# A two-cell recurrence on one core: normalization written in two halves, the cells' states summed ahead of the output product, and another order of a step

## The chip, the core and the metric

The program runs on one core of a Trainium2 chip. The metric is the device time of one execution in microseconds (us). The kernel before takes 3012.37 us, the median of three runs (3011.68 to 3013.71). The profiled execution spans 3003.6 us.

## What is computed

An image of 256 x 256 positions with 32 channels goes through four layers: a gated attention layer over an axis of length one (so that its softmax falls away), two Sobel layers, and a recurrence. The change touches the recurrence alone. It runs along the width: 256 steps t, over 256 sequences (one per row of the image), with two cells stacked (l = 0 and 1) of 128 hidden units:

```
z = x_t @ W_lat + b_lat
for j in range(2):
    zz = concatenate([z, h_all[j]]) @ W_cell[j] + b_cell[j]
    zz = group_norm(zz)            # 4 groups of 128: i, f, o, g
    i, f, o, g = split(zz, 4)
    c = sigmoid(f) * c_all[j] + sigmoid(i) * tanh(g)
    h = sigmoid(o) * tanh(c)
    z = z + h
x_hat = x_t + z @ W_out + b_out
```

Since z is the projected input plus h of both cells, x_hat needs (h0 + h1) @ W_out, and the rest is a product of x_t alone.

## The kernel before

The 256 sequences are held in two halves of 128 (h = 0 and 1), since a tile has 128 partitions. A **unit** is one cell on one half, written (l,h); a step has four units: (0,0), (0,1), (1,0), (1,1). A mean that group normalization would subtract is taken out of the weights beforehand, so what is left per unit is a mean square of each of the four groups and a division. The operations of a unit, by the names that the plan gives them and their lines in the profile:

- x (L702, TensorE, two products): the input's share of zz, for this unit of cell 1 and for a unit of cell 0 one or two steps on. i (L713): for cell 1, h of cell 0 in the same step times weights. m (L718): the unit's own h of the step before times weights. Each of i and m is 128x128 by 128x512 in float32, recorded as two matmul instructions.
- sq (L726, ScalarE): squares of zz, 512 columns. rd (L731, VectorE): their sums by group. pw (L734, GpSimd): the power -1/2 of 4 numbers per partition.
- nz (L738, VectorE): zn = zz times the four factors, 512 columns, out of the accumulator memory (PSUM).
- sg (L754, ScalarE): the sigmoid of i, f and o, 384 columns. tg (L756, ScalarE): the tanh of g.
- ig (L759, VectorE): c = i times g. fc (L763, GpSimd): f times the old c. c (L767, VectorE): c = c + fc, in place.
- th (L771, ScalarE): tanh of c. h (L774, VectorE): o times that. T (L777, TensorE): h transposed. e (L782): the copy out of PSUM into hT, on VectorE for cell 0 and on ScalarE for cell 1.

So every unit goes through TensorE, ScalarE, VectorE, GpSimd, VectorE, ScalarE, VectorE (with GpSimd beside it), ScalarE, VectorE and TensorE once per step, and the four units are staggered, so that each engine works on one unit while the others wait for another engine. The order in which the instructions stand in each engine's queue is written out by hand: PLAN gives each operation a time within the step, PERIOD is the distance of two steps, all operations of all 256 steps are sorted by time and emitted in that order. These times are not enforced on the chip. An engine takes its instructions strictly in the order of its queue, each as soon as what it waits for is there. In a planned time above PERIOD, the operation belongs to an earlier step than the one that runs at the same moment.

The output is written for blocks of four steps (emit, four parts, one per step): part 0 multiplies x_t of the block into px (L788); part 1 adds the four products of hT of cell 0 with W_out (L792); part 2 the four of cell 1, and then fin, ScalarE's copy of px with a bias (L801); part 3 transposes fin (pf, L808), VectorE copies that (st, L809), and every fourth block is stored. The emission stands at 0.90 of the step in the plan: after m(0,0) on TensorE, between sg(0,1) and tg(0,1) on ScalarE, and between c(1,0) and rd(1,1) on VectorE.

There is a second arm of the program for scales and shifts of the normalization that are not 1 and 0; with these inputs the first one (`plain`) runs.

Of the kernel before, what the change touches and what calls it, by code (L numbers as in the profile page):

```python
# [10 lines left out]
F32 = mybir.dt.float32  # L11
AF = mybir.ActivationFunctionType
# [4 lines left out]
S = 256  # L17
T = 256
C = 32
J = 4  # L20
NB = T // J
P = 128
H = 128
L = 2
# [490 lines left out]
def recurrent_weights(  # L515
# [114 lines left out]

PERIOD = 8.82
PLAN = {
    (0, 0): dict(m=0.0, sq=1.64, rd=2.4, pw=3.16, nz=4.25, sg=5.29, tg=5.72, fc=5.89, ig=6.1, c=6.55),
    (0, 1): dict(m=4.5, sq=6.14, rd=6.81, pw=7.57, nz=8.66, sg=9.61, tg=10.04, fc=10.21, ig=10.51),
    (1, 0): dict(x=10.17, i=11.42, m=12.42, sq=13.58, rd=14.3, pw=15.16, nz=16.47, sg=17.22, tg=17.65),
    (1, 1): dict(x=14.22, i=15.64, m=16.74, sq=17.9, rd=18.71, pw=19.48, nz=20.88, sg=21.63, tg=22.06),
}
PLAN[0, 0].update(th=6.9, h=7.43, T=7.8, e=8.27)  # L640
PLAN[0, 1].update(c=10.96, th=11.31, h=11.84, T=12.3, e=12.68)
PLAN[1, 0].update(fc=17.82, ig=18.1, c=18.45, th=19.07, h=19.56, T=20.12, e=20.48)
PLAN[1, 1].update(fc=22.23, ig=22.51, c=22.86, th=23.57, h=23.97, T=24.34, e=24.75)
EMIT = 27.36


def recurrence(tc, xa, out_nat, ident, weights, plain):

    nc = tc.nc
    wc, fx, gam, bet, e4, cst4, wout = weights  # L650
    XT = 2
    NX = 3
    ctx = ExitStack()
# [16 lines left out]

    up = ctx.enter_context(tc.tile_pool(name="unit", bufs=5))
    sp = ctx.enter_context(tc.tile_pool(name="state", bufs=2))
    hp = ctx.enter_context(tc.tile_pool(name="hid", bufs=10))
    op = ctx.enter_context(tc.tile_pool(name="outp", bufs=2))
    ps_zz = ctx.enter_context(tc.tile_pool(name="ps_zz", bufs=1, space=PSUM))
    ps_h = ctx.enter_context(tc.tile_pool(name="ps_h", bufs=2, space=PSUM))
# [2 lines left out]
    v = {}  # L679
    todo = []  # L680

    def at(when, what, *args):
        todo.append((when, len(todo), what, args))
# [10 lines left out]
    def project(l, h, t):  # L694

        if t >= T:
            return
        zz = v["zz", l, h] = ps_zz.tile([P, 4 * H], F32, name=f"zz{l}{h}")
        blk, j = divmod(t, J)
        rows = slice(l * X1, l * X1 + KX)  # L700
        x = xts[blk // XT % NX][rows, blk % XT, j, h * P : (h + 1) * P]
        nc.tensor.matmul(zz, lhsT=x, rhs=fx[rows, l, :], start=True, stop=l == 0 and t == 0)  # L702

    def one(name, l, h, t):
        seqs = slice(h * P, (h + 1) * P)
        get = lambda k: v[k, l, h]
        gates = lambda x, g: x[:, g * H : (g + 1) * H]
        four = lambda x: x.rearrange("p (g m) -> p g m", g=4)
        if name == "x":
            project(0, 1 - h, t + 1 + h)  # L710
            project(1, h, t)
        elif name == "i":
            nc.tensor.matmul(  # L713
                get("zz"), lhsT=v["hT", 0, t][:, seqs], rhs=wc[:, l, 0, :], start=False, stop=t == 0
            )
        elif name == "m":
            if t:
                nc.tensor.matmul(  # L718
                    get("zz"),
                    lhsT=v["hT", l, t - 1][:, seqs],  # L720
                    rhs=wc[:, l, 1, :],
                    start=False,
                    stop=True,
                )
        elif name == "sq":
            nc.scalar.activation(  # L726
                sqs[l, h][:, :, 0:H], four(get("zz")), AF.Square, scale=float(H**-0.5)
            )
        elif name == "rd":
            ve = v["ve", l, h] = up.tile([P, 4], F32, name="ve")  # L730
            nc.vector.tensor_reduce(ve, sqs[l, h], AX.X, ALU.add)  # L731
        elif name == "pw":
            rs = v["rs", l, h] = up.tile([P, 4], F32, name="rs")
            nc.gpsimd.tensor_tensor(rs, get("ve"), mhalf, ALU.pow)  # L734
        elif name == "nz":
            zn = v["zn", l, h] = up.tile([P, 4 * H], F32, name="zn")
            if plain:
                nc.vector.tensor_mul(  # L738
                    four(zn), four(get("zz")), get("rs").unsqueeze(2).to_broadcast([P, 4, H])
                )  # L740
                return
            for g in range(4):
                nc.vector.scalar_tensor_tensor(
                    gates(zn, g),
                    gates(get("zz"), g),
                    get("rs")[:, g : g + 1],
                    gates(gam[:, l, :], g),
                    ALU.mult,
                    ALU.mult,
                )  # L750
            nc.vector.tensor_add(zn, zn, bet[:, l, :])
        elif name == "sg":
            ga = v["ga", l, h] = up.tile([P, 4 * H], F32, name="ga")
            nc.scalar.activation(ga[:, 0 : 3 * H], get("zn")[:, 0 : 3 * H], AF.Sigmoid)  # L754
        elif name == "tg":
            nc.scalar.activation(gates(get("ga"), 3), gates(get("zn"), 3), AF.Tanh)  # L756
        elif name == "ig":
            c = v["cn", l, h] = sp.tile([P, H], F32, name=f"c{l}{h}")
            nc.vector.tensor_mul(c, gates(get("ga"), 0), gates(get("ga"), 3))  # L759
        elif name == "fc":  # L760
            if t:
                fc = v["fc", l, h] = up.tile([P, H], F32, name="fc")
                nc.gpsimd.tensor_mul(fc, gates(get("ga"), 1), get("c"))  # L763
        elif name == "c":
            c = get("cn")
            if t:
                nc.vector.tensor_add(c, c, get("fc"))  # L767
            v["c", l, h] = c
        elif name == "th":
            th = v["th", l, h] = up.tile([P, H], F32, name="th")  # L770
            nc.scalar.activation(th, get("c"), AF.Tanh)  # L771
        elif name == "h":
            hh = v["h", l, h] = up.tile([P, H], F32, name="h")
            nc.vector.tensor_mul(hh, gates(get("ga"), 2), get("th"))  # L774
        elif name == "T":
            pt = v["pt", l, h] = ps_h.tile([P, 4 * H], F32, name="pt")
            nc.tensor.transpose(pt[:, 0:P], get("h"), ident)  # L777
        elif name == "e":
            if h == 0:
                v["hT", l, t] = hp.tile([P, S], F32, name=f"hT{l}")  # L780
            copy = nc.scalar.copy if l else nc.vector.tensor_copy
            copy(v["hT", l, t][:, seqs], get("pt")[:, 0:P])  # L782

    def emit(blk, part):

        if part == 0:
            px = v["px"] = ps_x.tile([P, S], F32, name="px")
            nc.tensor.matmul(px, lhsT=e4, rhs=xa[:, blk, :], start=True, stop=False)  # L788
        elif part < 1 + L:
            l = part - 1  # L790
            for j in range(J):
                nc.tensor.matmul(  # L792
                    v["px"][j * C : (j + 1) * C, :],
                    lhsT=wout,
                    rhs=v.pop(("hT", l, blk * J + j)),
                    start=False,
                    stop=l == L - 1,
                )
            if l == L - 1:
                fin = v["fin"] = op.tile([P, S], F32, name="fin")  # L800
                nc.scalar.activation(fin, v["px"], AF.Identity, bias=cst4)  # L801
        else:
            if blk % 4 == 0:
                v["st"] = op.tile([P, 2, 4, P], F32, name="st")
            st = v["st"]
            pf = ps_x.tile([P, 2, P], F32, name="pf")
            for half in range(2):
                nc.tensor.transpose(pf[:, half, :], v["fin"][:, half * P : (half + 1) * P], ident)  # L808
            nc.vector.tensor_copy(st[:, :, blk % 4, :], pf)  # L809
            if blk % 4 == 3:  # L810
                w0 = (blk - 3) * J
                for half in range(2):
                    nc.sync.dma_start(
                        out=out_nat[:, half, w0 : w0 + 4 * J, :].rearrange("p w c -> p (w c)"),
                        in_=st[:, half].rearrange("p b m -> p (b m)"),
                    )

    for k in range(NB // XT):
        at(((k - NX + 1) * XT * J + 2.0) * PERIOD if k >= NX else -1e6, load, k)
    for h in range(2):  # L820
        at(-1e5, project, 0, h, 0)
    at(PLAN[1, 1]["x"] - PERIOD, project, 0, 0, 1)
    for t in range(T):
        for (l, h), ops in PLAN.items():
            for name, when in ops.items():
                at(t * PERIOD + when, one, name, l, h, t)
    for blk in range(NB):
        for part in range(L + 2):
            at((blk * J + J - 1 + part) * PERIOD + EMIT, emit, blk, part)
    todo.sort(key=lambda e: e[:2])  # L830
    with tc.manual_schedule():
# [44 lines left out]
```

## Time and profile before

| what | us |
|---|---|
| span of the profiled execution | 3003.6 |
| first normalization of the recurrence starts | 689.93 |
| last h of the recurrence | 2992.48 |
| one step on average: nz(0,0) of step 0 to step 255, 689.93 to 2973.61, by 255 | 8.956 |
| in 740 to 1500 us: TensorE busy | 733.26 of 760 |
| VectorE busy | 698.68 |
| ScalarE busy | 528.11 |
| GpSimd busy | 498.03 |

Steps are not equally long. From the starts of nz(0,0), steps 40 to 239, by the place of the step in its block of four (t mod 4), medians:

| from step t to t + 1, t mod 4 = | us | what of the emission falls in it |
|---|---|---|
| 1 | 8.59 | part 0 |
| 2 | 8.61 | part 1 |
| 3 | 9.48 | part 2 |
| 0 | 9.09 | part 3 |

The sum, 35.77 us a block, is what the recurrence is made of 64 times. In the profile "idle before" an instruction is the time that its engine stood still ahead of it, and behind the arrow stands what it waited for. The duration of an instruction on VectorE or ScalarE is longer than the distance to the next start: instructions that need not wait for each other overlap.

### The profile page before, as it was taken

Reading aid. Unit: us, or ns where it says so; the run is one execution under the profiler, and the core shown is the slowest. Engines: PE = TensorE matmul, PEld = TensorE weight load, DVE = VectorE, ACT = ScalarE, POOL = GpSimd, SP = SyncE. Lnnn points to the kernel's source line nnn. Section 1 sums busy time; section 2 is a strip of 40 time slices with the busy share of each in tenths; the row PEclk is TensorE's granted clock in tenths of the full one; section 3 lists DMA queues with packets and bytes.
Section 4 is the critical chain, followed back from the end, with each engine's and each line's share of the span. In section 5 each row is a group of like instructions: output and inputs, shape, how many; then the busy total and the mean of one; then the engine's idle time right before and its main releaser. Section 6 shows DMA issues by size and latency. Waiting matters only on the chain.

```text
span 3003.6 us, 39237 instructions
## 1 busy us (share of the span) xinstructions
PE 2830.3 (94%) x10209; PEld 1042.6 (35%) x10209; DVE 2646.4 (88%) x6572; ACT 1986.9 (66%) x5393; POOL 1718.6 (57%) x2272
## 2 busy tenths in 40 slices
PE   7899898988999999999999999999999999999997
PEld 4433333332333333333333333333333333333332
DVE  5778798986999999999999999999999999999997
ACT  5355486755666666676666766676666666666665
POOL 2300055636666666666666666666666666666665
PEclk9899999988999999999999999999999999999999
DMA  3000000001000000000000000000000000000000
GB/s 128 1 1 1 1 1 1 1 15 24 11 16 8 15 9 15 8 15 8 15 8 15 8 16 7 17 15 8 16 8 15 10 16 8 16 8 15 1 8 9
DMA packets 29314, 38.42 MB, mean 13 GB/s; under 512 B 5732, under 2 KB 22149, under 8 KB 29080
## 3 DMA queue, kind: packets, MB, share of 16 engines
q1 hardware_dynamic: 27392, 33.57, 3.9%
q8 instruction: 84, 1.38, 0.2%
q10 hardware_dynamic: 888, 1.95, 0.2%
q14 instruction: 150, 1.23, 0.1%
q0 software_dynamic: 800, 0.30, 0.0%
HBM read 10.63 MB, written 8.39 MB: 6 GB/s over the span
## 4 chain that ended last, share of the span: by engine, by line
PE 42%; DVE 39%; POOL 10%; issue 4%; ACT 2%; DVEq 0%; POOLq 0%; ACTq 0%
DVE ve L731 13%; PE zz L718 11%; POOL rs L734 9%; DVE zn L738 8%; PE zz L713 7%; DVE c L759 6%; DVE c L767 6%; PE pv L277 4%; PE pt L777 4%; PE pg L440 4%; PE pg L400 3%; PE px L792 2%; PE zz L702 2%; PE pg L302 2%; DVE h L774 2%
## 5 line engine op out<-in xcount | busy, mean ns | idle before, releaser
L734 POOL TENSOR_TENSOR rs<-ve,mhalf 128x4 f32<-128x4 f32 x1024 | 1036.6, 1012 | 281.5 <-DVE ve L731 237.1
L718 PE MATMUL zz<-wc,hT 128*128 128x512 f32 x2040 | 962.6, 594 | 1.2 <-DVE hT L782 1.2
L754 ACT ACTIVATE ga<-zn 128x384 f32<-128x384 f32 x1024 | 531.3, 519 | 468.0 <-DVE zn L738 467.5
L738 DVE TENSOR_TENSOR zn<-zz,rs 128x512 f32<-128x512 f32 x1024 | 701.1, 685 | 84.7 <-POOL rs L734 76.6
L763 POOL TENSOR_TENSOR fc<-ga,c 128x128 f32<-128x128 f32 x1020 | 466.8, 458 | 522.4 <-ACT ga L754 522.4
L731 DVE TENSOR_REDUCE ve<-sq 128x4 f32<-128x516 f32 x1024 | 697.2, 681 | 16.6 <-POOL sq L669 14.1
L726 ACT ACTIVATE sq<-zz 128x512 f32<-128x512 f32 x1024 | 606.3, 592 | 26.6 <-PE zz L718 14.3
L702 PE MATMUL zz<-fx,xt 33*128 33x512 f32 x2048 | 584.8, 643 | 11.5 <-DVE zn L738 8.2
L713 PE MATMUL zz<-wc,hT 128*128 128x512 f32 x1024 | 525.3, 595 | 0.0
L718 PEld LDWEIGHTS zz<-wc,hT 128*128 128x128 f32 x2040 | 359.6, 196 | 264.6 <-DVE hT L782 213.7
L771 ACT ACTIVATE th<-c 128x128 f32<-128x128 f32 x1024 | 311.4, 304 | 182.6 <-DVE c L767 177.9
L777 PEld LDWEIGHTS pt<-ident,h 128*128 128x128 f32 x1024 | 141.9, 139 | 804.8 <-DVE h L774 710.2
L777 PE MATMUL pt<-ident,h 128*128 128x128 f32 x1024 | 321.7, 314 | 87.6 <-DVE h L774 79.2
L767 DVE TENSOR_TENSOR c<-c,fc 128x128 f32<-128x128 f32 x1020 | 291.2, 286 | 55.9 <-DVE c L759 2.3
L759 DVE TENSOR_TENSOR c<-ga 128x128 f32<-128x128 f32 x1024 | 302.9, 296 | 38.7 <-ACT ga L756 38.6
L756 ACT ACTIVATE ga<-zn 128x128 f32<-128x128 f32 x1024 | 303.2, 296 | 0.0
L774 DVE TENSOR_TENSOR h<-ga,th 128x128 f32<-128x128 f32 x1024 | 292.0, 285 | 0.8 <-ACT th L771 0.8
L702 PEld LDWEIGHTS zz<-fx,xt 33*128 33x128 f32 x2048 | 156.1, 185 | 298.4 <-PE zz L718 226.3
L288 ACT ACTIVATE sg<-pg 128x512 f32<-128x512 f32 x256 | 132.1, 602 | 110.8 <-PE pg L277 110.8
L713 PEld LDWEIGHTS zz<-wc,hT 128*128 128x128 f32 x1024 | 183.3, 219 | 2.3 <-issue 2.3
L393 POOL TENSOR_TENSOR dh<-pp 128x512 f32<-128x512 f32 x64 | 99.4, 1553 | 115.6 <-DVE pp L380 98.9
L296 DVE TENSOR_TENSOR o<-pv,sg 128x512 f32<-128x512 f32 x256 | 155.4, 678 | 4.4 <-ACT sg L288 4.1
(147 smaller groups left out, 2306.8 us busy)
## 6 DMA issues: line engine op xcount, KB each, us to landing
xt<-xa SPq DMA_DIRECT2D x256, 64.0 KB, 2.0
nat<-in_x_dram SPq DMA_DIRECT2D x16, 512.0 KB, 8.3
out_dram<-st SPq DMA_DIRECT2D x32, 256.0 KB, 2.3
wc<-in_L_conv_W_cell_dram ACTq DMA_DIRECT2D x2, 512.0 KB, 4.1
kt<-in_consts_dram ACTq DMA_DIRECT2D x1, 832.0 KB
wv<-in_L_conv_Wv_dram POOLq DMA_DIRECT2D x4, 32.0 KB, 4.8
wg<-in_L_conv_Wg_dram POOLq DMA_DIRECT2D x4, 32.0 KB, 6.6
gamma<-in_L_conv_ln_gamma_dram POOLq DMA_DIRECT2D x4, 0.1 KB, 6.1
```

Of the source, the lines that this page charges most:

```text
L702: nc.tensor.matmul(zz, lhsT=x, rhs=fx[rows, l, :], start=True, stop=l == 0 and t == 0)
L713: nc.tensor.matmul(get("zz"), lhsT=v["hT", 0, t][:, seqs], rhs=wc[:, l, 0, :], start=False, stop=t == 0)
L718: nc.tensor.matmul(get("zz"), lhsT=v["hT", l, t - 1][:, seqs], rhs=wc[:, l, 1, :], start=False, stop=True,)
L726: nc.scalar.activation(sqs[l, h][:, :, 0:H], four(get("zz")), AF.Square, scale=float(H**-0.5))
L731: nc.vector.tensor_reduce(ve, sqs[l, h], AX.X, ALU.add)
L734: nc.gpsimd.tensor_tensor(rs, get("ve"), mhalf, ALU.pow)
L738: nc.vector.tensor_mul(four(zn), four(get("zz")), get("rs").unsqueeze(2).to_broadcast([P, 4, H]))
L754: nc.scalar.activation(ga[:, 0 : 3 * H], get("zn")[:, 0 : 3 * H], AF.Sigmoid)
L759: nc.vector.tensor_mul(c, gates(get("ga"), 0), gates(get("ga"), 3))
L763: nc.gpsimd.tensor_mul(fc, gates(get("ga"), 1), get("c"))
L767: nc.vector.tensor_add(c, c, get("fc"))
L777: nc.tensor.transpose(pt[:, 0:P], get("h"), ident)
```

## The change

Three things are changed, and the plan's numbers with them. The split is to let the gates begin on the first half of a unit's normalization, and to give the planner smaller pieces to place; the sum is to take products off TensorE and put an addition on GpSimd, which has more idle time.

- The normalization nz is written as two instructions of 256 columns: nz for the gates i and f, and n2 for o and g. The sigmoid is split in the same way: sg now takes i and f (256 columns), and a new so takes o (128 columns).
- A new hs on GpSimd adds hT of both cells (128x256), once per step. The output product then takes the sum: four products a block in place of eight, and the emission has three parts: x_t's product; the four products with fin behind them; the transposition with st.
- The plan has been made anew: PERIOD 8.74 for 8.82, and another order. On VectorE, ig of another unit stands between nz and n2 at two of the four places, and hT of cell 0 needs fewer buffers (6 for 10).

```
-PERIOD = 8.82
+PERIOD = 8.74
...
+        def half(i):
+            g = slice(2 * i, 2 * i + 2)
+            nc.vector.tensor_mul(
+                four(get("zn"))[:, g, :],
+                four(get("zz"))[:, g, :],
+                get("rs")[:, g].unsqueeze(2).to_broadcast([P, 2, H]),
+            )
...
+        elif name == "n2":
+            if plain:
+                half(1)
         elif name == "nz":
             zn = v["zn", l, h] = up.tile([P, 4 * H], F32, name="zn")
             if plain:
-                nc.vector.tensor_mul(
-                    four(zn), four(get("zz")), get("rs").unsqueeze(2).to_broadcast([P, 4, H])
-                )
+                half(0)
                 return
...
-            nc.scalar.activation(ga[:, 0 : 3 * H], get("zn")[:, 0 : 3 * H], AF.Sigmoid)
+            nc.scalar.activation(ga[:, 0 : 2 * H], get("zn")[:, 0 : 2 * H], AF.Sigmoid)
+        elif name == "so":
+            nc.scalar.activation(gates(get("ga"), 2), gates(get("zn"), 2), AF.Sigmoid)
...
+    def both(t):
+        hs = v["hs", t] = hp.tile([P, S], F32, name="hs")
+        nc.gpsimd.tensor_add(hs, *[v.pop(("hT", l, t)) if l else v["hT", l, t] for l in range(L)])
...
-                    rhs=v.pop(("hT", l, blk * J + j)),
+                    rhs=v.pop(("hs", blk * J + j)),
```

One half of a step in VectorE's queue, by the plans (a digit pair is the unit):

```
before: rd00 h01 nz11         e01 nz00 ig11      c11 rd10 ig00 h11 c00 | rd01
after:  rd00 h01 nz11 n2(11)  e01 nz00 ig11 n2(00) c11 rd10 ig00 h11 c00 | rd01
```

The other half is the same with the units rd01, h00, nz10, n2(10), e00, nz01, ig10, n2(01), c10, rd11, ig01, h10, c01. GpSimd's queue for one step is after the change: hs, fc01, pw11, pw00, fc11, fc00, pw10, pw01, fc10.

More of the change, by code (lines that the diff above doesn't have):

```diff
@@ L627, in recurrent_weights @@
     return (wc, fx, gam, bet, e4, cst4, wout), plain
-PERIOD = 8.82
+PERIOD = 8.74
 PLAN = {
[L635 to L638, printed above, removed]
-}
[L640 to L644, printed above, removed]
+    (0, 0): dict(m=0.0, sq=1.54, rd=2.37, pw=3.12, nz=4.21, n2=4.79, sg=5.28, tg=5.6, fc=5.76),
+    (0, 1): dict(m=4.47, sq=6.02, rd=6.74, pw=7.5, nz=8.59, n2=9.16, sg=9.54, tg=9.87, fc=10.03),
+    (1, 0): dict(x=9.98, i=11.34, m=12.35, sq=13.48, rd=14.14, pw=14.95, nz=16.32, n2=16.66),
+    (1, 1): dict(x=14.08, i=15.52, m=16.61, sq=17.75, rd=18.52, pw=19.27, nz=20.68, n2=21.04),
+}
+PLAN[0, 0].update(ig=6.03, c=6.47, so=6.56, th=6.83, h=7.36, T=7.72, e=8.28)
+PLAN[0, 1].update(ig=10.39, so=10.82, c=10.85, th=11.2, h=11.72, T=12.2, e=12.64)
+PLAN[1, 0].update(sg=16.8, tg=17.16, fc=17.29, so=17.36, ig=17.68, c=18.25, th=18.82, h=19.36)
+PLAN[1, 1].update(sg=21.18, tg=21.52, fc=21.66, so=21.73, ig=22.05, c=22.62, th=23.29, h=23.73)
+PLAN[1, 0].update(T=19.93, e=20.29)
+PLAN[1, 1].update(T=24.11, e=24.52, hs=26.48)
+EMIT = 27.09
 def recurrence(tc, xa, out_nat, ident, weights, plain):
@@ L672, in recurrence @@
     sp = ctx.enter_context(tc.tile_pool(name="state", bufs=2))
-    hp = ctx.enter_context(tc.tile_pool(name="hid", bufs=10))
+    hp = ctx.enter_context(tc.tile_pool(name="hid", bufs=6))
     op = ctx.enter_context(tc.tile_pool(name="outp", bufs=2))
@@ L774, in one @@
             nc.vector.tensor_mul(hh, gates(get("ga"), 2), get("th"))
+        elif name == "hs":
+            both(t)
         elif name == "T":
@@ L788, in emit @@
             nc.tensor.matmul(px, lhsT=e4, rhs=xa[:, blk, :], start=True, stop=False)
-        elif part < 1 + L:
-            l = part - 1
+        elif part == 1:
             for j in range(J):
@@ L794, in emit @@
                     lhsT=wout,
-                    rhs=v.pop(("hT", l, blk * J + j)),
+                    rhs=v.pop(("hs", blk * J + j)),
                     start=False,
-                    stop=l == L - 1,
+                    stop=True,
                 )
-            if l == L - 1:
-                fin = v["fin"] = op.tile([P, S], F32, name="fin")
-                nc.scalar.activation(fin, v["px"], AF.Identity, bias=cst4)
+            fin = v["fin"] = op.tile([P, S], F32, name="fin")
+            nc.scalar.activation(fin, v["px"], AF.Identity, bias=cst4)
         else:
@@ L827, in recurrence @@
     for blk in range(NB):
-        for part in range(L + 2):
+        for part in range(3):
             at((blk * J + J - 1 + part) * PERIOD + EMIT, emit, blk, part)
```

## The prediction

> **What bounds the kernel now.** I read the busy shares first, then the costliest groups, then the recurrence in order of time, and last the length of each step by its place in the block.
>
> ```profile
> PE 2830.3 (94%) x10209; PEld 1042.6 (35%) x10209; DVE 2646.4 (88%) x6572; ACT 1986.9 (66%) x5393; POOL 1718.6 (57%) x2272
> ...
> L734 POOL TENSOR_TENSOR rs<-ve,mhalf 128x4 f32<-128x4 f32 x1024 | 1036.6, 1012 | 281.5 <-DVE ve L731 237.1
> ...
> L738 DVE TENSOR_TENSOR zn<-zz,rs 128x512 f32<-128x512 f32 x1024 | 701.1, 685 | 84.7 <-POOL rs L734 76.6
> ```
>
> No engine is idle for long, but nz waits for the power, and the power for rd. The timeline of VectorE and GpSimd over one undisturbed half step shows how these interlock:
>
> ```profile
> 2158.46 0.69 DVE L738 TENSOR_TENSOR zn<-zz,rs 128x512 f32<-128x512 f32 x1 [0.19 <-POOL rs L734]
> ...
> 2159.07 0.28 DVE L759 TENSOR_TENSOR c<-ga 128x128 f32<-128x128 f32 x1
> ...
> 2159.45 0.29 DVE L767 TENSOR_TENSOR c<-c,fc 128x128 f32<-128x128 f32 x1
> ...
> 2159.66 0.68 DVE L731 TENSOR_REDUCE ve<-sq 128x4 f32<-128x516 f32 x1
> ...
> 2160.26 0.28 DVE L759 TENSOR_TENSOR c<-ga 128x128 f32<-128x128 f32 x1
> ...
> 2160.46 0.30 DVE L774 TENSOR_TENSOR h<-ga,th 128x128 f32<-128x128 f32 x1
> 2160.69 0.28 DVE L767 TENSOR_TENSOR c<-c,fc 128x128 f32<-128x128 f32 x1
> ...
> 2160.82 0.33 PE L777 MATMUL pt<-ident,h 128*128 128x128 f32 x1 [0.19 <-DVE h L774]
> ...
> 2160.89 0.68 DVE L731 TENSOR_REDUCE ve<-sq 128x4 f32<-128x516 f32 x1
> ...
> 2161.71 1.01 POOL L734 TENSOR_TENSOR rs<-ve,mhalf 128x4 f32<-128x4 f32 x1 [0.28 <-DVE ve L731]
> ...
> 2162.75 0.69 DVE L738 TENSOR_TENSOR zn<-zz,rs 128x512 f32<-128x512 f32 x1 [0.19 <-POOL rs L734]
> ```
>
> This is a closed loop of 4.29 us: nz to ig 0.61, ig to its c 0.38 (c waits for ig's result; unrelated small instructions start 0.20 apart), c to rd 0.21, rd to ig 0.60, ig to h 0.20, h to c 0.23, c to rd 0.20, then rd to nz by way of GpSimd 1.86. Twice that is 8.58; the undisturbed step has 8.59. So VectorE's queue with one power in it bounds a quiet step. TensorE is close behind: it stands still ahead of the transposition (0.19 here), and adding the starts (i 0.86, T about 0.15, m 0.86 twice, the two x products 1.06 and 0.09 ahead of them) gives some 4.05 a half, 8.1 a step.
>
> A block lasts 35.77 us, 4 x 8.59 is 34.36: emission costs 1.41 a block. Where it falls:
>
> ```profile
> 2155.20 0.47 ACT L801 ACTIVATE fin<-px,cst 128x256 f32<-128x256 f32 x1 [0.45 <-PE px L792]
> ...
> 2155.90 0.29 DVE L759 TENSOR_TENSOR c<-ga 128x128 f32<-128x128 f32 x1 [0.57 <-ACT ga L756]
> ```
>
> ```profile
> 2163.71 0.38 PE L808 MATMUL pf<-ident,fin 128*128 128x128 f32 x2
> ...
> 2163.75 0.29 DVE L767 TENSOR_TENSOR c<-c,fc 128x128 f32<-128x128 f32 x1
> ...
> 2164.12 0.43 DVE L809 COPY st<-pf 128x256 f32<-128x256 f32 x1
> ...
> 2164.47 0.68 DVE L731 TENSOR_REDUCE ve<-sq 128x4 f32<-128x516 f32 x1
> ```
>
> fin waits in ScalarE's queue for the output products with tg(0,1) behind it, and ig(0,1) waits for tg: pw(0,0) comes 2.01 us after pw(1,1) there (2155.41, 2157.42) in place of 1.29, so 0.72. Then st: c to rd takes 0.72 in place of 0.21, so 0.5: 0.35 its own slot, the rest the wait for pf. The remaining 0.19 is the first set of products (0.57 to 0.61 on TensorE, mostly inside its slack).
>
> [...] this trace has 1036 ns for an add of 512 columns (L389) and 458 for a product of 128 (L763).
>
> **The change, part by part.**
>
> Two halves of nz: [...] st, also 256 columns out of PSUM, has 425 in the trace, and 0.35 to the next start. So I take 0.34 a half: 0.68 in place of 0.61, 0.07 more, 0.28 a step of VectorE. It is on VectorE's queue, but only nz(0,0) and nz(0,1) lie on the loop. Those of (1,1) and (1,0) fall into the wait for the power (0.19 idle today, and they take 0.07 of it).
>
> On the loop: nz to ig 0.34 in place of 0.61 (ig of the other unit needs only its own tg, due before), ig to n2 0.20, n2 to c 0.34. Together nz to c 0.88 in place of 0.99, as n2 lies where c waited for ig. Minus 0.11 a half, 0.22 a step. In this place ig must find tg of (1,1) done: n2(11) ends about 0.75 after nz(11) starts, tg 0.10 + 0.30 later, ig stands 1.40 after it. Enough. A quiet step is 8.59 - 0.22 = 8.37.
>
> Sigmoid in two: [...] so stands behind tg and waits for nothing; h, which needs it, comes over 1 us later. On the path: zero, hidden by ScalarE's idle time. tg gains a wait for n2; behind it stand th and sq of other units, which come no later than before, as nz starts the chain 0.27 earlier.
>
> hs: by L763 and L389, 458 + 128 x (1036-458)/384 = 0.65 us; by the dearer L393 (1553 ns at 512 columns) 0.82. It stands between fc(1,0) and fc(0,1), where GpSimd is idle 0.68 us now (the wait of fc for sg). Behind it queue fc(0,1), for which c(0,1) waits, and pw(1,1). From the end of pw(0,1): 0.46 + 0.82 + 0.46 with gaps of 0.05 to 0.1 ends some 1.95 later; rd(1,1) ends about then. Zero at 0.65 to 0.82; at 1.1 us it would cost 0.2 a step.
>
> Four products fewer: TensorE loses 0.57 a block. It costs 0.19 today, so 0.19 is gained, no more.
>
> The emission that stays meets a VectorE that is earlier against TensorE. fin still follows the four products, and these still follow m(0,0), which comes only about 0.1 earlier in its half (e(0,0) waits for the same h), while tg(0,1) could start some 0.1 to 0.2 earlier than now. I put fin's step at 0.87 (0.72 before). st likewise: c(1,0) comes some 0.2 earlier, pf at most 0.1, so 0.65 (0.50 before). x_t's product, 0.43 on TensorE and free today, meets a slack of 8.37 - 8.1 = 0.27 instead of 0.5: 0.15. Emission: 0.15 + 0.87 + 0.65 = 1.67, against 1.41.
>
> Sum: 4 x 8.37 + 1.67 = 35.15 a block, 0.62 less than 35.77; times 64 is 40 us. 3012 - 40 = 2972; I say 2973.
>
> **Rivals.** (a) TensorE becomes the bound and eats the gain. It needs 4 x 8.1 + 0.43 + 0.57 + 0.23 = 33.6 a block; it can't make up a delay of fin or st when it has no slack, and small waits (hs late, x waiting for n2 to release zz) add up. If the block gets about 35.4, the gain is 22: 2990. For it: TensorE busy 733 of 760. Against: it stands still ahead of T in each half. (b) The emission does not grow, since the products come sooner: 4 x 0.22 + 0.19 = 1.07 a block, 68 us: 2944. For it: the removed products stood in the step ahead of fin. Against: fin's own wait is for products of its own step. (c) Slower: ig does not find tg in time, or hs holds up fc and pw, so that the 0.28 of VectorE are paid and nothing is hidden: 0.2 to 0.3 a step, half made up by the products: about +35, 3047. For it: VectorE gets more work, 92% busy. Against: the wait that n2 fills is in the timeline.
>
> **Chances.** The forecast 0.53, (a) 0.25, (b) 0.12, (c) 0.10. Range: the forecast's unknown costs (0.34 to 0.36 a half of nz, fin and st 0.15 either way) make about 15 us each way; leaving out (c) and the outer part of (b) gives 2949 to 3000. Faster by over 0.2% (6 us) 0.88, within 0.03, slower 0.09.
>
> **What would show it.** Two zn groups of about 425 ns each with 0.34 to the next start; nz to c 0.88; quiet steps of 8.37 and the steps with fin and st 0.85 and 0.65 longer; hs under 0.85 us, and no wait of c for fc. It is wrong if quiet steps stay at 8.59 (then the loop is another one), if c waits for GpSimd, or if T no longer waits for h (TensorE bound).

## The result, and the profile after

The changed kernel takes 2977.36 us (median of 4 runs, 2976.93 to 2980.28), the kernel before 3012.02 us on the same chip: a ratio of 0.9887, 95% interval 0.9869 to 0.9904. It is 34.7 us faster. 2973 was predicted, with 2949 to 3000 as the range. The profiled execution spans 2975.1 us.

The page's first part and four groups of the changed kernel, in the columns of the page before (busy, mean ns | idle before it):

```profile
PE 2814.5 (95%) x9697; PEld 1026.9 (35%) x9697; DVE 2695.6 (91%) x7596; ACT 2114.2 (71%) x6417; POOL 1948.8 (66%) x2528
...
L745 POOL TENSOR_TENSOR rs<-ve,mhalf 128x4 f32<-128x4 f32 x1024 | 1069.0, 1044 | 289.2 <-DVE ve L742 250.3
...
L714 DVE TENSOR_TENSOR zn<-zz,rs 128x256 f32<-128x256 f32 x2048 | 812.5, 417 | 66.3 <-POOL rs L745 4.7
...
L781 DVE TENSOR_TENSOR c<-c,fc 128x128 f32<-128x128 f32 x1020 | 338.5, 332 | 1.4 <-DVE h L788 0.5
...
L803 POOL TENSOR_TENSOR hs<-hT,hT 128x256 f32<-128x256 f32 x256 | 219.9, 859 | 2.1 <-ACT hT L798 2.1
```

VectorE's and GpSimd's shares have grown, TensorE has 512 matmuls fewer. The half of the normalization takes 417 ns, where the prediction took about 425 from st. One row is not as expected: c takes 332 ns on average, 286 before, although nothing about c was changed. The timeline of the half step in which the addition hs runs (VectorE and GpSimd) shows where that is:

```profile
1767.37 0.42 DVE L714 TENSOR_TENSOR zn<-zz,rs 128x256 f32<-128x256 f32 x1
...
1767.71 0.28 DVE L773 TENSOR_TENSOR c<-ga 128x128 f32<-128x128 f32 x1
1767.72 0.86 POOL L803 TENSOR_TENSOR hs<-hT,hT 128x256 f32<-128x256 f32 x1
...
1767.90 0.42 DVE L714 TENSOR_TENSOR zn<-zz,rs 128x256 f32<-128x256 f32 x1
...
1768.24 0.49 DVE L781 TENSOR_TENSOR c<-c,fc 128x128 f32<-128x128 f32 x1
...
1768.64 0.46 POOL L777 TENSOR_TENSOR fc<-ga,c 128x128 f32<-128x128 f32 x1
1768.65 0.68 DVE L742 TENSOR_REDUCE ve<-sq 128x4 f32<-128x516 f32 x1
```

From nz over ig and n2 to c it is 0.87 us (ig lasts 0.28, and n2 starts 0.19 behind it), where the prediction worked out 0.88 and the kernel before took 0.99. But c(1,0) starts in time and then lasts 0.49 in place of 0.28, until just after hs is done, and rd begins 0.41 behind c in place of 0.20.

The lengths of the steps, as in the table of the kernel before (medians, steps 40 to 239):

| t mod 4 | before, us | after, us | emission after |
|---|---|---|---|
| 0 | 9.09 (st) | 8.51 | none |
| 1 | 8.59 | 8.51 | x_t's product |
| 2 | 8.61 | 9.26 | four products, fin |
| 3 | 9.48 (fin) | 8.94 | pf, st |
| sum | 35.77 | 35.22 | |

With the irregular steps the block is 35.83 before and 35.27 after: 0.56 less, times 64 is 36 us. The wait of fin and the place of st in the changed kernel, ScalarE and VectorE in the timeline:

```profile
1812.96 0.47 ACT L820 ACTIVATE fin<-px,cst 128x256 f32<-128x256 f32 x1 [0.63 <-PE px L812]
...
1813.67 0.29 DVE L773 TENSOR_TENSOR c<-ga 128x128 f32<-128x128 f32 x1 [0.57 <-ACT ga L770]
```

```profile
1821.25 0.49 DVE L781 TENSOR_TENSOR c<-c,fc 128x128 f32<-128x128 f32 x1
1821.33 0.38 PE L827 MATMUL pf<-ident,fin 128*128 128x128 f32 x2
...
1821.75 0.42 DVE L828 COPY st<-pf 128x256 f32<-128x256 f32 x1
...
1822.09 0.68 DVE L742 TENSOR_REDUCE ve<-sq 128x4 f32<-128x516 f32 x1
```

fin holds up tg and with it ig(0,1), as before: fin waits 0.63 for the products, tg, next in ScalarE's queue, starts 0.38 behind fin (at 1813.34), and VectorE idles 0.57 ahead of ig. c to rd with st between is 0.84, against 0.41 without it.

### The profile page after: what moved, and what is told of

It reads as the page before. It is cut to its first block, busy times and chain, and to the rows that moved or that the text cites. A ratio compares the mean times of both kernels' runs of the same rounds, so it can differ in the third digit from the quotient of the medians.

```text
span 2975.1 us, 41024 instructions
## 1 busy us (share of the span) xinstructions
PE 2814.5 (95%) x9697; PEld 1026.9 (35%) x9697; DVE 2695.6 (91%) x7596; ACT 2114.2 (71%) x6417; POOL 1948.8 (66%) x2528
## 4 chain that ended last, share of the span: by engine, by line
PE 50%; DVE 27%; POOL 15%; issue 4%; ACT 2%; DVEq 0%; POOLq 0%; DMA 0%; ACTq 0%
POOL rs L745 14%; PE zz L729 14%; DVE ve L742 8%; PE zz L724 7%; PE zz L704 7%; DVE c L781 5%; DVE zn L714 4%; PE pv L277 4%; PE pt L793 4%; PE pg L440 4%; DVE c L773 3%; PE pg L400 3%; PE pg L302 2%; PE px L812 2%; PE pg L277 1%
## 5 line engine op out<-in xcount | busy, mean ns | idle before, releaser
L745 POOL TENSOR_TENSOR rs<-ve,mhalf 128x4 f32<-128x4 f32 x1024 | 1069.0, 1044 | 289.2 <-DVE ve L742 250.3
L714 DVE TENSOR_TENSOR zn<-zz,rs 128x256 f32<-128x256 f32 x2048 | 812.5, 417 | 66.3 <-POOL rs L745 4.7
L766 ACT ACTIVATE ga<-zn 128x256 f32<-128x256 f32 x1024 | 422.0, 412 | 383.8 <-DVE zn L714 383.8
L781 DVE TENSOR_TENSOR c<-c,fc 128x128 f32<-128x128 f32 x1020 | 338.5, 332 | 1.4 <-DVE h L788 0.5
L773 DVE TENSOR_TENSOR c<-ga 128x128 f32<-128x128 f32 x1024 | 289.4, 283 | 37.9 <-ACT ga L770 37.9
L768 ACT ACTIVATE ga<-zn 128x128 f32<-128x128 f32 x1024 | 305.3, 298 | 0.0
L770 ACT ACTIVATE ga<-zn 128x128 f32<-128x128 f32 x1024 | 303.3, 296 | 0.3
L704 PEld LDWEIGHTS zz<-fx,xt 33*128 33x128 f32 x2048 | 162.5, 185 | 326.6 <-PE zz L729 278.0
L803 POOL TENSOR_TENSOR hs<-hT,hT 128x256 f32<-128x256 f32 x256 | 219.9, 859 | 2.1 <-ACT hT L798 2.1
```

The source lines that it names most:

```text
L714: nc.vector.tensor_mul(four(get("zn"))[:, g, :], four(get("zz"))[:, g, :], get("rs")[:, g].unsqueeze(2).to_broadcast([P, 2, H]),)
L766: nc.scalar.activation(ga[:, 0 : 2 * H], get("zn")[:, 0 : 2 * H], AF.Sigmoid)
```

## The experiments

**Theory A:** hs on GpSimd holds up a VectorE instruction that runs beside it; this is 0.2 us in every step. **Theory B:** c(1,0) is long for a reason of its own place in the new order. The steps' lengths and the durations of c, by unit, decide between them. All runs are summed up in a table at the end of this section.

**Without the addition** (cell 1's share of the output is left out, and hT has its 10 buffers again):

```
-PLAN[1, 1].update(T=24.11, e=24.52, hs=26.48)
+PLAN[1, 1].update(T=24.11, e=24.52)
-                    rhs=v.pop(("hs", blk * J + j)),
+                    rhs=v.pop(("hT", 0, blk * J + j)),
```

> The changed kernel without the addition hs: the output products take cell 0's states alone, so cell 1's share of the output is left out (four products a block, as in the changed kernel). Theory A (the addition on GpSimd holds up the c of unit (1,0) that runs beside it, 0.49 us for 0.28, and so every step): c(1,0) back to 0.28, quiet steps 8.30 for 8.51, 0.84 a block less, of which emission may take back up to 0.4: 2925 to 2950. Theory B (c(1,0) is long for a reason of its own place, such as fc's result coming late or the read behind n2): c(1,0) stays at 0.48, quiet steps 8.51, 2977.

Measured: 2956.33 us; c(1,0) 0.28, undisturbed steps 8.29. The same half step in the timeline of this run:

```profile
1757.78 0.42 DVE L714 TENSOR_TENSOR zn<-zz,rs 128x256 f32<-128x256 f32 x1
...
1758.12 0.28 DVE L773 TENSOR_TENSOR c<-ga 128x128 f32<-128x128 f32 x1
...
1758.32 0.42 DVE L714 TENSOR_TENSOR zn<-zz,rs 128x256 f32<-128x256 f32 x1
...
1758.66 0.28 DVE L781 TENSOR_TENSOR c<-c,fc 128x128 f32<-128x128 f32 x1
...
1758.86 0.69 DVE L742 TENSOR_REDUCE ve<-sq 128x4 f32<-128x516 f32 x1
```

This is theory A. The time, 2956, lies just above the range of 2925 to 2950, as fin's step grew to 9.38 and st's stayed at 8.94: emission costs 1.74 a block here, 1.18 in the changed kernel.

**The addition moved** to behind fc(1,1):

```
-PLAN[1, 1].update(T=24.11, e=24.52, hs=26.48)
+PLAN[1, 1].update(T=24.11, e=24.52, hs=30.46)
```

> The addition, whole, moved in GpSimd's queue from behind fc(1,0) to behind fc(1,1). Theory A: the long c moves with it: c(1,1) 0.45 to 0.5 us, c(1,0) 0.28; the time within 10 us of 2977. Theory B: c(1,0) stays at 0.48 and c(1,1) at 0.28.

Measured: c(1,1) 0.48, c(1,0) 0.28: the long c moves with the addition, theory A. The undisturbed step stays at 8.51. The time was a miss, 3002.13 us: the steps with fin and st are 9.46 and 9.17 there, 0.20 and 0.23 more. In the changed kernel the hold-up falls in the same half step as fin and st, and here it does not.

**The sum undone** (eight products in two steps, no addition; the emission and the 10 buffers of hT are those of the kernel before, all else as changed):

> The sum undone, the rest of the change kept: no addition, eight products a block in the four parts of the kernel before, the normalization in halves and the new order as they are. Theory A: quiet steps 8.30; the four products more cost 0.2 to 0.5 a block: 2930 to 2955, so the sum is a loss. Theory B: quiet steps 8.51, and the products cost 0.2 a block: about 2990, so the sum is a gain.

Measured: 2977.41 us, the changed kernel's time. Undisturbed steps 8.29 as theory A had it, but the block is 35.29: steps of 8.59 for the first four products and 9.44 for the others with fin. So four products cost 0.36 a block (35.29 less 34.93 of the run without addition), 21 us in all, and the addition costs the same 21 us (2977.36 less 2956.33). The sum as a whole brings nothing; the halves and the order bring the 35.

**The sum alone, in the order of the kernel before:** the emission and `both` as changed, `hs=26.70`, the rest of before.py.

> The kernel before with the sum alone (addition behind fc(1,0), four products, three parts), the normalization whole and the old order. Theory A: c(1,0), which runs beside the addition, takes 0.45 to 0.5, the step is 0.2 longer, the products give back 0.2 a block: 3012 + 64 x 0.6 = 3050. Theory B: 3012 - 12 = 3000.

Measured: 3059.89 us, 1.6% slower than before (ratio 1.0161, 1.0144 to 1.0178). c(1,0) takes 0.63, more than expected, and the undisturbed step 8.93.

**ig behind n2:** is it the halves or the order that brings the gain?

```
-... nz=4.21, n2=4.79 ...      -... nz=8.59, n2=9.16 ...
+... nz=4.21, n2=4.50 ...      +... nz=8.59, n2=8.87 ...
```

> The changed kernel with ig put behind n2 instead of between nz and n2, in both halves of the step; all else kept. If it is the order that brings the gain (the second half of the normalization fills c's wait for ig), nz to c becomes 0.34 + 0.34 + 0.38 = 1.06 for 0.88: 0.18 longer in the half of nz(0,0), 0 to 0.18 in the half of nz(0,1), where c(1,0) is held up by the addition anyway: quiet steps 8.69 to 8.87, 3015 to 3065. If the halves alone bring it (gates that begin earlier): quiet steps 8.51, 2977.

Measured: 3122.03 us and undisturbed steps of 9.24, well beyond the range expected. nz to c(1,1) is 1.06, as expected. In the other half ig(1,0) has now come to lie beside the addition as well, and c(1,0) beside fc (VectorE and GpSimd in the timeline):

```profile
1835.47 0.73 POOL L803 TENSOR_TENSOR hs<-hT,hT 128x256 f32<-128x256 f32 x1
1835.80 0.56 DVE L773 TENSOR_TENSOR c<-ga 128x128 f32<-128x128 f32 x1
1836.40 0.45 POOL L777 TENSOR_TENSOR fc<-ga,c 128x128 f32<-128x128 f32 x1 [0.20 <-ACT ga L766]
1836.46 0.54 DVE L781 TENSOR_TENSOR c<-c,fc 128x128 f32<-128x128 f32 x1
```

Each of the two ends some 0.15 after the GpSimd instruction beside it. To see the order alone, the same was done without the sum:

> As the run with the sum undone, and ig behind n2 in both halves: the halves in an order that fills no wait, and no addition that could hold up a VectorE instruction. If the gain is the order's: nz to c 1.06 for 0.87 in both halves, quiet steps 8.67 for 8.29, 3005 to 3040, about the kernel before or worse. If the halves alone bring something: quiet steps under 8.5, below 2990.

Measured: 3026.21 us, ratio 1.0053 (1.0037 to 1.007), undisturbed steps 8.71. Halves in an order that fills no wait make the kernel slower than before; with ig between them they take 49 us off that. The gain is the order's, and the halves are what makes the order possible.

**Any GpSimd instruction, or one with two inputs?** A copy with one input in place of the addition, cell 1's states written three times so that it lasts long enough (cell 0's share of the output is left out):

```
-        nc.gpsimd.tensor_add(hs, *[...])
+        nc.gpsimd.tensor_copy(three, v.pop(("hT", 1, t)).unsqueeze(1).to_broadcast([P, 3, S]))
```

> At the addition's place GpSimd makes a copy with one input instead, of cell 1's states, written three times (768 columns) so that it lasts 0.8 us or more; the products take the copy, so cell 0's share of the output is left out. If any long GpSimd instruction holds up c(1,0): c(1,0) 0.45 us or more, and ends some 0.15 after the copy. If only one with two inputs does: c(1,0) 0.28, quiet steps 8.30 as long as the copy stays under 0.95 us (a longer one delays fc(0,1) and pw(1,1) instead).

Measured: c(1,0) 0.58, undisturbed steps 8.60, 3008.98 us; two steps of its timeline:

```profile
1792.61 0.97 POOL L804 COPY hs<-hT 128x768 f32<-128x768 f32 x1
1792.61 0.28 DVE L773 TENSOR_TENSOR c<-ga 128x128 f32<-128x128 f32 x1
1793.14 0.58 DVE L781 TENSOR_TENSOR c<-c,fc 128x128 f32<-128x128 f32 x1
...
1801.86 0.83 POOL L804 COPY hs<-hT 128x768 f32<-128x768 f32 x1
1801.86 0.97 DVE L773 TENSOR_TENSOR c<-ga 128x128 f32<-128x128 f32 x1
```

Two inputs on GpSimd are not needed. Where ig and the copy start together, either ig is done in 0.28 and the copy lasts 0.97, or the copy is done in 0.83 and ig lasts 0.97: it looks as if one has to wait for the other.

**fin later**, behind e(1,0), where ScalarE is idle (0.64 us ahead of sg at 1771.18 in the trace of the changed kernel):

```
+        at((blk * J + J) * PERIOD + EMIT + 2.03, finish, blk)
```

> The changed kernel with fin, ScalarE's copy of the output products, put 2.03 us later in the plan, behind the copy e(1,0), where ScalarE idles; the products stay. If fin's wait with tg(0,1) behind it is what the step with fin pays: that step 8.6 to 8.8 for 9.26, the block 0.45 to 0.65 shorter, 2935 to 2950. If the four products on TensorE are what it pays: 9.2, and 2970 to 2977.

Measured: 2938.16 us, and the step with fin 8.53 for 9.26: fin's place in ScalarE's queue is what that step paid for, hardly the products.

**The addition in halves** of 128 columns, behind fc(1,1) and fc(1,0):

```
-PLAN[1, 1].update(T=24.11, e=24.52, hs=26.48)
+PLAN[1, 1].update(T=24.11, e=24.52, ha=21.90, hs=26.48)
```

> The addition in two halves of 128 columns: one behind fc(1,1), the other behind fc(1,0), each to be over (0.46 us) when the next c begins. Theory A: all four c at 0.28, quiet steps 8.30 to 8.35, 2950 to 2962 like the run without the addition. If the addition costs by its work rather than by which VectorE instruction it meets: quiet steps 8.45 to 8.51, 2970 to 2977.

Measured: 2960.26 us, all four c at 0.28, undisturbed steps 8.29. The addition costs by what it meets, not by its work (twice 0.59 us here).

**Everything together:** the addition in halves, fin later, and st copied by ScalarE (`EMIT + 6.33`):

> The addition in halves, fin later, and the copy st on ScalarE (6.33 us later in the plan, where it idles) together. Quiet steps 8.30, no hold-up by fin or st: then TensorE's own work, some 33.6 us a block, is the next limit: 33.7 to 34.3 a block, 2885 to 2925. If the hold-ups are made good elsewhere: 34.8 or more, 2955.

Measured: 2882.34 us, ratio 0.9568 to the kernel before (0.9552 to 0.9584), the fastest version found. The stretch from 740 to 1500 us (busy us and instructions by engine, TensorE's clock, DMA):

```profile
740.00:1500.00 760.00, 758.88 (x2432) 274.84 (x2432) 735.75 (x2340) 606.25 (x2026) 635.58 (x901) 1.00 0.04 12
```

TensorE is busy 758.88 of 760 us, and TensorE's work makes up 93% of the chain that ended last (from 1000 to 2700 us; 45% in the changed kernel). So now it is nearly the bound: a block takes 33.80 against the 33.6 that the prediction added up from its starts. In this state the sum should be worth something, which the last run asks:

> The version with fin later and st on ScalarE, with the sum undone (eight products in two steps, no addition). It asks what the sum is worth once the hold-ups are gone. If TensorE is the limit there: 0.36 to 0.57 a block more than the version with the sum, 2882 + 23 to 37: 2905 to 2920. If the sum is still neutral: 2882.

Measured: 2902.64 us, 20 more and 0.30 a block; a little under the range, but clearly no longer neutral. Four products more on TensorE make 33.6 + 0.57 = 34.17 by the prediction's figures, and the block takes 34.10. Here the chain is TensorE's to 100%. The run before it was still 0.2 above its own 33.6, which fits that the products cost 0.30 and not 0.57.

| run | us | undisturbed step | block | c(1,0) |
|---|---|---|---|---|
| before | 3012 | 8.59 | 35.83 | 0.29 |
| changed | 2977.36 | 8.51 | 35.27 | 0.49 |
| without addition | 2956.33 | 8.29 | 34.93 | 0.28 |
| addition moved | 3002.13 | 8.51 | 35.68 | 0.28 |
| sum undone | 2977.41 | 8.29 | 35.29 | 0.28 |
| sum alone | 3059.89 | 8.93 | 36.56 | 0.63 |
| ig behind n2 | 3122.03 | 9.24 | 37.54 | 0.55 |
| the same, sum undone | 3026.21 | 8.71 | 36.05 | 0.29 |
| copy for addition | 3008.98 | 8.60 | 35.73 | 0.58 |
| fin later | 2938.16 | 8.51 | 34.65 | 0.48 |
| addition in halves | 2960.26 | 8.29 | 35.03 | 0.28 |
| everything | 2882.34 | 8.30 | 33.80 | 0.28 |
| everything, sum undone | 2902.64 | 8.30 | 34.10 | 0.28 |

(The undisturbed steps of the last two are the shortest of the block, 8.29 to 8.31.)

## Why the prediction was right, and where it was not

The time was met within 5 us, but that was luck: two terms of the sum were off in opposite directions. The undisturbed step was put 0.14 too short, 0.56 a block, and the emission 0.49 a block too dear. One of the prediction's own signs of being wrong, that c waits for GpSimd, came true, if not in the way it meant (c waiting for fc).

- **The loop.** Right. A half of nz costs 0.34 to the next start, nz to c is 0.87 to 0.88, rd to nz by way of GpSimd 1.86 as before. Without the addition the step is 8.29, better than the 8.37 worked out, since c to rd (0.20) and ig to the second rd (0.61) also came out 0.01 to 0.02 shorter. That the order does it, and not the halves, is shown by the two runs with ig behind n2.
- **hs costs nothing.** This is the step that failed. The prediction followed only those who queue behind hs on GpSimd, fc(0,1) and pw(1,1), and these indeed did not delay anyone. It did not ask which VectorE instruction runs beside it. c(1,0) does, and pays 0.20 in each step, which becomes 0.22 longer. The size was close too: 0.86 us for 0.65 to 0.82, part of it probably hs itself waiting for ig, as it lasts 0.73 where it does not start together with ig.
- **Four products fewer bring 0.19 a block, no more.** Undersized for the new order: 0.36, by the run with the sum undone and the run without the addition (the former also spreads its emission over one step more). Nor was the 0.19 of the kernel before what the prediction took it for; see below the list.
- **The emission costs 1.67.** It was 1.18 in the changed kernel (fin 0.75, st 0.43, x_t's product nothing), but 1.74 in the run without the addition (fin 1.09, st 0.65). So the sum fits a VectorE that is not held up, though not its parts: fin 1.09 for 0.87, x_t's product nothing for 0.15. The hold-up falls just ahead of fin's and st's places, so that part of their wait is over when VectorE comes there. With the addition moved to the other half step, st costs 0.66 again and fin 0.95. For the same reason taking the addition away brings 21 us and not the 0.21 x 255 = 54 that the single step suggests.
- **The sigmoid in two** costs nothing on the path: right, the loop's terms are unchanged and h waits for so nowhere (VectorE idles 1.1 us ahead of h in the whole trace, all of it for th). ScalarE pays for it: sg and so take 412 and 298 ns where sg took 519, and with its other instructions it is busy 2114.2 us for 1986.9, 0.5 a step.
- **Rival (a)**, TensorE as the bound, did not come about: TensorE stands still for 22.9 of 760 us in the changed kernel, and the step shortens to 8.29 when the addition alone goes. It nearly came about when the hold-ups were gone. The sign that the prediction names, T waiting for h, does not tell the two apart: over 1000 to 2800 us the weight load of T waits 644.9 us for h in the changed kernel, and still 484.7 with everything together. Its starts, as listed, give 3.88 a half; the 4.05 is right with the second transposition of the half. A block of 35.4 would be a gain of 24 us, not 22. **Rival (b)** would have needed fin out of the way. **Rival (c)** named hs, but by way of fc and pw behind it in GpSimd's queue; in the sum alone, 48 us slower, it is c that is held up. Its "half made up by the products" does not follow from the 0.19 a block that the prediction gives them against 0.8 to 1.2 of cost.

The hold-up already stands in the profile of the kernel before (GpSimd and VectorE, from the step t mod 4 = 3, which ends with fin):

```profile
2150.65 0.46 POOL L763 TENSOR_TENSOR fc<-ga,c 128x128 f32<-128x128 f32 x1 [0.97 <-ACT ga L754]
...
2150.80 0.45 DVE L759 TENSOR_TENSOR c<-ga 128x128 f32<-128x128 f32 x1
...
2151.18 0.28 DVE L774 TENSOR_TENSOR h<-ga,th 128x128 f32<-128x128 f32 x1
```

ig(0,0), 0.28 elsewhere, takes 0.45 beside fc and ends 0.14 after it, and h starts 0.38 behind it in place of 0.20. This is so in this step of 61 of the 64 blocks. It also answers where the prediction's remaining 0.19 went: by the table of steps, the step with the first four products is only 0.02 longer than a quiet one, but fin's step 0.89, of which fin's wait is 0.72. The other 0.17 is this hold-up. Whether the products bring it about, by delaying sg and so fc, is not shown.

The profiles differ by 28.5 us, the times by 34.7: the profiled execution of the kernel before took 3005.52 us, 6.5 less than its median. In it TensorE's clock is granted in full from 702 us on, in the profile of the changed kernel from 716 (0.50 from 695 to 715, against 0.81 before), and there the second step of the recurrence takes 13.48 us for 8.95: 4.5 us that come once. The change is not shown to be the reason. All eleven experiments have this long step, and single executions of the kernel before lie between 3004.4 and 3014.5 us.

## What to carry to other kernels

Where queues are planned by hand, write down the closed loop of waits with the distances between starts, and look for work of another unit that fits into a wait on that loop; splitting an instruction paid here only where the pieces fill such a wait (without the sum 2977 us with ig between the halves, 3026 with ig behind them, 3012 before). For work moved to an engine that is idle, ask not only who queues behind it there but also which instruction of another engine runs beside it (here c, 0.20 longer in each step). What one removes from one place can come back in part at the next wait (without the addition 21 us were gained of the 54 that the single step suggests), so price a change by the block, not by the step.

## What the hardware showed that was not expected

In these runs, GpSimd instructions over 128 to 768 columns (fc, hs, the copy) and two VectorE instructions with two SBUF inputs (c and ig) hold each other up: c takes 0.49 beside hs for 0.28, ig 0.45 beside fc for 0.28 in the kernel before, and the copy 0.97 for 0.83 where ig is done first. In the trace of the changed kernel, c takes 0.485 beside hs (196 of the 200 steps from 40 to 239), 0.281 beside pw and 0.281 beside nothing; n2, which reads PSUM and four numbers, takes 0.418 with and without hs beside it; rd, with one SBUF input, 0.68 both beside fc and without. The VectorE instruction that is held ends 0.14 to 0.16 us after the GpSimd instruction, an addition, a product or a copy alike. What brings this about in the two engines is not shown. What was not tried is a VectorE instruction with one SBUF input in c's place. pw, over 1 us long but on four columns, is a case of its own: for unit (1,0) of the changed kernel, where h starts 0.04 behind it, either pw takes 1.19 for 1.01 and h 0.28, or pw keeps its 1.01 and h takes 0.30. Why it holds up nobody by more than that was not tested.
